# Two more products by Strassen's seven multiplications, and late roots by Heron's rule, in a two-layer graph network with an eigen-solver

## The chip, the cores and the metric

The kernel runs on one core of a Trainium2 chip. Its time is the device time of one execution in microseconds (us), and smaller is better. PE is the matrix engine (TensorE), DVE is VectorE, ACT is ScalarE, POOL is GpSimd, SP is the engine that issues most of the DMAs.

## The reference

Everything is float32. `x` holds 64 graphs of 256 nodes with 256 features, and all share one 256x256 matrix `adj`. Two blocks follow each other, each with a layer norm and a relu in front and a residual sum behind.

```python
# layer 0
G = adj * adj
h = relu(layernorm(x))
h = relu(G @ (h @ W1))        # W1 256x512
h = relu(G @ (h @ W2))        # W2 512x1024
x = x + G @ (h @ W3)          # W3 1024x256
# layer 1
h = relu(layernorm(x))
A  = adj;  deg = A.sum(0) + A.sum(1) - diag(A);  dinv = deg ** -0.5
_, U = eigh(dinv[:, None] * (diag(deg) - A) * dinv[None, :])
h = relu((U.T @ h) @ V1 + b1)  # V1 256x128
x = x + U @ (h @ V2 + b2)      # V2 128x256
```

The second block needs all eigenvectors U of one symmetric 256x256 matrix, which depends on `adj` alone.

## The kernel before

**Layer 0** goes over 32 pairs of graphs. For a pair q the class `Layers` issues, on PE: `first` (G^T h), `widened` (W1), `spread_by_seven` (G), `third_by_seven` (W2, as a 2x2 block product with Strassen's seven products in place of eight), `fourth` (W3: 32 matmuls of 128x128 by 128x256 into two held PSUM banks, over the eight 128-row blocks of `s2`), `last` (G on the result `p3`), then, after the residual sum and the second layer norm, `turn_rows` (eight transposes) and `for_layer1` (h V1, called hw). The residual row and hw of each pair are spilled to DRAM. ACT copies the products out of PSUM and does the relus (`rectify` does those on `s2`), POOL issues DMAs that add in flight and computes the norms' inverse roots with its power operation. `products` writes the order of a pair's work down; parts of neighbouring pairs are interleaved in it.

**The eigen-solver** (`Eigen`) runs beside layer 0 as one long dependent chain, mostly on DVE, with help of ACT, POOL and PE: a Householder reduction to tridiagonal form until about 1300 us, leaves of 16 by QL steps until about 1660, and then four levels of divide and conquer (32, 64, 128, 256) until about 2137. In each level `rational_steps` finds the new eigenvalues, as many in parallel as there are columns: a starting value, then `ROOT_STEPS` = 5 rational steps, each with a quadratic formula whose square root `power(dq, dq, 0.5)` is computed on POOL (`rdq` in the profile), six per level and 24 in all:

```python
            self.ts(dq, dq, 1e-36, OP.max)
            self.power(dq, dq, 0.5)
            self.tt(b, b, dq, OP.add)
            self.recip(b, b)
```

**The order on the engines** is made when the program is built. Layer 0 and layer 1 are generators (`streams`), the solver calls its instructions one by one, and `Pace` holds a model of each engine's clock. When the solver has an instruction for PE or ACT, `Pace.run` first issues whatever of the streams can begin before that instruction is due. The order of PE and ACT is then fixed, and in the levels that of POOL too (`pool_too`, in `join`). A stream can yield a condition (a lambda), and it goes on only when that holds in the plan. On the chip each engine works off its list in order and waits with semaphores for data.

**Layer 1** begins when U is there. A flag from the solver is read, a branch is taken (`mend`, which would repeat the last phase of the solver), and then for each pair: hw and the row are fetched by SP, `to_vectors` computes U^T hw (four matmuls of 128x128 by 128x256 per pair), DVE adds b1, ACT applies the relu, POOL makes `xb`, the row plus U's row sums times b2; `from_vectors` multiplies with U and `finish` with V2, DVE adds `xb` and SP writes the output. `layer1_of` runs these three pairs deep.

Most lines of the profile carry L210, the line of the helper that issues all calls, so groups are told apart by tile names: `s` is `s2` (numbers are left out of names), `L_gnn_W` a weight, `forms` and `sums` belong to the W2 product.

Of the kernel before, what the change touches and what calls it, by code (L numbers as in the profile page):

```python
# [29 lines left out]
H = 2  # L30
PAIRS = 32
SEVEN_FROM = 1
FLAG_US = 3.5
LN_EPS = 1e-5
EPS = 2.0**-24
# [6 lines left out]
QL_QUICK = 32  # L42
QL_LATE = 30
ROOT_STEPS = 5
ROOT_LAST = 2.0**-8
EXP_STEPS = [64, 32, 16, 8, 4, 2, 1]
MANT_BITS = 23
# [238 lines left out]
class Eigen:  # L286
# [947 lines left out]
    def rational_steps(self, n, kd, zsum, zown, znxt, acc, s, gap, half, y, bs, rb):  # L1234
# [33 lines left out]
        for step in range(ROOT_STEPS):  # L1268
            self.tt(x, y, s, OP.mult)
            for h in range(H):  # L1270
                self.ts(bs[:, h, :], kd[:, h, :], x[:, h : h + 1], OP.subtract)
            self.recip(rb, bs)
            if wide:
                for i in range(3):
                    for h in range(H):
                        a = rb if i == 0 else t
                        c = zsum if i == 0 else rb
                        self.stt(
                            t[:, h, 0:n], a[:, h, :] if i == 0 else a[:, h, 0:n], 1.0, c[:, h, :],
                            OP.mult, OP.mult, accum=sums[:, i, h : h + 1],  # L1280
                        )
            else:
                tv = t.rearrange("p h n -> p (h n)")[:, 0 : 3 * H * n].rearrange("p (i h n) -> p i h n", i=3, h=H)
                self.tt(tv[:, 0], rb, zsum, OP.mult)
                self.tt(tv[:, 1], tv[:, 0], rb, OP.mult)
                self.tt(tv[:, 2], tv[:, 1], rb, OP.mult)
                nc.vector.tensor_reduce(
                    sums.rearrange("p i h -> p (i h)"), tv.rearrange("p i h n -> p (i h) n"), AX.X, OP.add
                )
            self.tt(w, gap, y, OP.subtract)  # L1290
            self.tt(dd, w, y, OP.subtract)
            self.tt(m, y, w, OP.mult)
            self.tt(ms, m, s, OP.mult)
            self.ts(low, y, 2.0**-5, OP.mult)

            fv, g, b, c, c1, c2, dq = (f(k) for k in ("rf", "rg", "rb1", "rc", "rc1", "rc2", "rdq"))
            self.stt(fv, sums[:, 0], 1.0, s, OP.add, OP.mult)
            self.tt(g, fv, m, OP.mult)
            self.tt(c, fv, dd, OP.mult)
            self.tt(c1, dd, sums[:, 1], OP.mult)  # L1300
            self.tt(b, m, sums[:, 1], OP.mult)
            self.tt(c1, fv, c1, OP.subtract)
            self.tt(c2, ms, sums[:, 2], OP.mult)
            self.tt(b, b, c, OP.add)
            self.tt(c1, c1, c2, OP.subtract)
            self.tt(c2, b, b, OP.mult)
            self.tt(c1, c1, g, OP.mult)
            self.stt(dq, c1, 4.0, c2, OP.mult, OP.add)
            self.ts(dq, dq, 1e-36, OP.max)
            self.power(dq, dq, 0.5)  # L1310
            self.tt(b, b, dq, OP.add)
            self.recip(b, b)
            self.tt(g, g, b, OP.mult)
            if step == ROOT_STEPS - 1:
                size, near = f("rsz"), f("rnear")
                self.ts(size, g, -1.0, OP.mult)
                self.tt(size, size, g, OP.max)
                self.ts(near, y, ROOT_LAST / 2, OP.mult)
                self.tt(near, size, near, OP.is_le)
            self.stt(y, g, -2.0, y, OP.mult, OP.add)  # L1320
            self.tt(y, y, low, OP.max)
            self.tt(y, y, half, OP.min)
# [456 lines left out]
class Layers:  # L1779


    def __init__(self, tc, ctx, ap, gt2, u, ut):
# [17 lines left out]
        self.parts = [self.s1.rearrange("p m b f -> p (m b) f")[:, 1:4], forms[:, 0:3]]  # L1800
        self.y2 = self.forms.rearrange("p a c n -> p (a c n)")[:, 0:2048].rearrange("p (c n) -> p c n", c=4)
        self.sums = pool.tile([P, 3, 2, 512], F32, name="sums")
        self.s2 = pool.tile([P, 2, 4, 2, N], F32, name="s2")
        self.p3 = pool.tile([P, H, 2 * N], F32, name="p3")
        self.x1 = pool.tile([P, H, 2, N], F32, name="x1")
# [35 lines left out]

    def open1(self, ctx):

        self.io1 = ctx.enter_context(self.tc.tile_pool(name="l1_io", bufs=5))
        self.op = ctx.enter_context(self.tc.tile_pool(name="l1_out", bufs=3))
        self.wp1 = ctx.enter_context(self.tc.tile_pool(name="l1_work", bufs=4))
        self.ps1 = ctx.enter_context(self.tc.tile_pool(name="l1_psum", bufs=4, space=PSUM))
# [61 lines left out]
        return self.wp.tile([P, H, 2, N], F32, tag=tag, name=tag)  # L1909

    def streams(self):
        return Stream(self.products()), Stream(self.rows())

    def products(self):

# [2 lines left out]
        for q in range(PAIRS):  # L1918
# [1 line left out]
            if q == SEVEN_FROM:  # L1920
                yield from self.fold_weights()
            last = self.last(q - 1) if q > 0 else iter(())
            for part in self.third_by_seven() if seven else self.third():
                if part is None:
                    yield from next(last, ())
                else:
                    yield part
            if more:
                yield from self.first(q + 1)
                yield from self.widened(0)  # L1930
                yield from self.widened(1)
            forms = iter(())
            if more:
                forms = self.spread_by_seven() if q + 1 >= SEVEN_FROM else self.spread_in_turn()
            turned = iter(())
            if q > 0:
                yield lambda: q - 1 in self.h1
                turned = self.turn_rows()
                for _ in range(8):
                    yield next(turned)  # L1940
            step = next(forms, iter(()))
            if seven:
                yield from self.rectify(0)
            for _ in range(4 if more else 0):
                yield next(step)
            yield from turned
            yield from step
            products = self.fourth()
            yield from next(products)
            if seven:  # L1950
# [138 lines left out]
    def fold_weights(self):  # L2089
# [14 lines left out]
        self.lhs = {1: a[0, 0], 2: a[0, 1], 3: f3, 4: a[1, 1], 5: f5, 6: f6, 7: a[1, 0]}  # L2104
        self.rhs = {1: 0, 5: 1, 4: 2, 7: 3, 3: 4, 2: 5, 6: 6}

    def seventh(self, ps, k, jj, start=False):
        for i in range(2):
            at = (2 * jj + i) * P
# [7 lines left out]
                    skip_group_check=not start,  # L2117
                )

    def third_by_seven(self):  # L2120


        act = self.nc.scalar.activation
# [15 lines left out]
        for k, to in ((1, 1), (6, 2), (5, 0)):  # L2139
            for jj in range(2):  # L2140
                yield from product("u", jj, k, s2[:, jj, to])
            if k != 5:
                yield None
        yield from part("z", 0, 7, 0)
        yield from part("y", 0, 2, 1)
# [19 lines left out]
    def fourth(self):  # L2165
# [26 lines left out]
        for m in range(H):  # L2192
            yield second_half(m)

    def last(self, q):

        nc, x1 = self.nc, self.x1
        def rows(m):
            ps = self.bank()
            yield from self.products_of(  # L2200
                ps, [(self.gt2[:, h, m * P : (m + 1) * P], self.p3[:, h, :]) for h in range(H)]
# [47 lines left out]
    def turn(self):  # L2249

        nc = self.now
        nc.vector.tensor_reduce(self.u1, self.u, AX.X, OP.add)
        for h in range(H):
            nc.vector.tensor_scalar(self.ub2[:, h, :], self.b2, self.u1[:, h : h + 1], None, OP.mult)

    def fetch(self, q):
        hw = self.io1.tile([P, H, 2, P], F32, tag="hw", name="hw1")
        x1 = self.io1.tile([P, H, 2, N], F32, tag="x", name="x1")
        yield self.nc.sync.dma_start(out=hw.rearrange("p h b k -> p (h b k)"), in_=self.spilled_hw[q])
        yield self.nc.sync.dma_start(out=x1.rearrange("p h b f -> p (h b f)"), in_=self.spilled[q])  # L2260
        self.fetched[q] = x1, hw

    def to_vectors(self, q):

        nc = self.nc
        x1, hw = self.fetched.pop(q)
        z = self.wp1.tile([P, H, 2, P], F32, tag="z", name="z")
        ps = self.bank1()
        for m in range(H):
            yield from self.products_of(  # L2270
                ps[:, m * N : (m + 1) * N],
                [
                    (self.u[:, h, m * P : (m + 1) * P], hw[:, h].rearrange("p b k -> p (b k)"))
                    for h in range(H)
                ],
            )
        yield nc.vector.tensor_tensor(
            z.rearrange("p h b k -> p (h b) k"),
            ps.rearrange("p (g k) -> p g k", k=P),
            self.b1.unsqueeze(1).to_broadcast([P, H * 2, P]),  # L2280
            OP.add,
        )
        s = self.wp1.tile([P, H, 2, P], F32, tag="s", name="s")
        yield nc.scalar.activation(s, z, AF.Relu)
        xb = self.wp1.tile([P, H, 2, N], F32, tag="xb", name="xb")
        for b in range(2):
            yield nc.gpsimd.tensor_tensor(xb[:, :, b, :], x1[:, :, b, :], self.ub2, OP.add)
        self.mid[q] = s, xb

    def from_vectors(self, q):  # L2290

        s, xb = self.mid.pop(q)
        g = self.wp1.tile([P, 2 * N], F32, tag="g", name="g")
        ps = self.bank1()
        for b in range(2):
# [1 line left out]
                ps[:, b * N : (b + 1) * N], [(s[:, m, b, :], self.ut[:, m, :]) for m in range(H)]  # L2297
            )
        yield self.nc.scalar.copy(g, ps)
        self.end[q] = g, xb  # L2300

    def finish(self, q):
        nc = self.nc
        g, xb = self.end.pop(q)
        out = self.op.tile([P, H, 2, N], F32, tag="out", name="out")
        for m in range(H):
            ps = self.bank1()
# [5 lines left out]
            yield nc.vector.tensor_tensor(flat(out)[:, m, :], flat(xb)[:, m, :], ps, OP.add)  # L2313
            yield nc.sync.dma_start(out=self.view(self.ap["out"], q)[:, m], in_=out[:, m])

    def layer1_of(self, ahead=3):

        ready = lambda q: lambda: q in self.through
        for i in range(PAIRS + 2 + ahead):
            if i < PAIRS:  # L2320
                yield ready(i)
                yield from self.fetch(i)
            if 0 <= i - ahead < PAIRS:
                yield from self.to_vectors(i - ahead)
            if 0 <= i - ahead - 1 < PAIRS:
                yield from self.from_vectors(i - ahead - 1)
            if 0 <= i - ahead - 2:
                yield from self.finish(i - ahead - 2)

    def layer1(self, pace):  # L2330


        with self.tc.manual_schedule():
            self.turn()
            self.due = True
            self.fetched, self.mid, self.end = {}, {}, {}
            pace.streams = *pace.streams, Stream(self.layer1_of())
            pace.finish()


# [66 lines left out]
```

## Time and profile before

| | us |
|---|---|
| median of 3 runs (lowest, highest) | 2330.01 (2328.76, 2330.02) |
| the profiled execution | 2329.52 |
| its span, from the first to the last instruction | 2327.7 |
| PE busy in the span | 2276.4 |
| DVE busy | 1972.7 |
| ACT busy | 1224.3 |
| POOL busy | 720.1 |

The granted clock of TensorE is 0.999 of full speed over the span. A PE share is the time in which matmuls run; the weight load (PEld) overlaps them. Each float32 matmul leaves two records, so a count of x16 in a row of matmuls is eight matmuls. A releaser (`<-`) is what an engine waited for last.

### The profile page before, as it was taken

To read this page: it belongs to the slowest core of one execution; us is meant where nothing else is said; L and a number is where in the kernel's file an instruction comes from. 1 tells how busy PE (TensorE), PEld (TensorE's weight loads), DVE (VectorE), ACT (ScalarE), POOL (GpSimd) and SP (SyncE) were. 2 spreads that over 40 slices of the span, in tenths; PEclk is the share of its full clock that TensorE was granted. 3 is DMA by queue.
4 is the path that set the end of the run, shared out by engine and by line. 5 is a ranking of instruction groups with operands and counts; after the bars stand their busy time and mean duration, and the time that the engine had idled before them with its cause. 6 is when DMAs were issued, how large, how long until landed. Compare 5 with 4: busy or idle time off the path is not lost. (4 is left out here: it accounts for less than half of the span.)

```text
span 2327.7 us, 40756 instructions
## 1 busy us (share of the span) xinstructions
PE 2276.4 (98%) x10686; PEld 1850.2 (79%) x10686; DVE 1972.7 (85%) x12008; ACT 1224.3 (53%) x3015; POOL 720.1 (31%) x1978
## 2 busy tenths in 40 slices
PE   7999999999999999999999899999999999999999
PEld 4688888788778878888888778778888888787888
DVE  7989999999998999999999999999887787873343
ACT  4355655455554555556655356555555555544322
POOL 3445544455554223222222011111111111111543
PEclk9999999999999999999999999999999999999999
DMA  3123232223223222323323123333332222224776
GB/s 127 23 60 73 64 69 60 55 60 69 65 60 70 60 63 56 72 65 69 73 60 73 37 64 73 73 68 65 73 73 64 66 65 58 63 55 114 235 254 202
DMA packets 70622, 183.25 MB, mean 79 GB/s; under 512 B 7920, under 2 KB 29040, under 8 KB 70384
## 3 DMA queue, kind: packets, MB, share of 16 engines
q0 software_dynamic: 18000, 89.92, 20.3%
q1 hardware_dynamic: 52384, 90.67, 11.3%
q8 instruction: 86, 1.41, 0.2%
q14 instruction: 152, 1.25, 0.2%
HBM read 65.48 MB, written 41.94 MB: 46 GB/s over the span
## 5 line engine op out<-in xcount | busy, mean ns | idle before, releaser
L210 PE MATMUL bank<-forms,L_gnn_W 128*128 128x256 f32 (+2 forms) x2104 | 489.1, 381 | 0.0
L210 PE MATMUL bank<-L_gnn_W,s 128*128 128x256 f32 (+1 forms) x2096 | 472.4, 375 | 4.1 <-ACT s L210 3.1
L210 PEld LDWEIGHTS bank<-forms,L_gnn_W 128*128 128x128 f32 x2104 | 391.2, 191 | 60.6 <-issue 11.7
L210 PEld LDWEIGHTS bank<-L_gnn_W,s 128*128 128x128 f32 x2096 | 389.4, 190 | 56.9 <-ACT s L210 6.1
L210 ACT ACTIVATE s<-bank 128x512 f32<-128x512 f32 (+1 forms) x485 | 281.2, 582 | 218.0 <-PE bank L210 214.7
L210 PE MATMUL bank<-forms,sums 128*128 128x256 f32 (+1 forms) x1524 | 348.3, 374 | 0.0
L210 PEld LDWEIGHTS bank<-forms,sums 128*128 128x128 f32 x1524 | 283.4, 190 | 58.2 <-issue 23.7
L210 PE MATMUL bank<-gt,s 128*128 128x256 f32 (+1 forms) x1062 | 247.2, 372 | 1.1 <-ACT s L210 0.7
L210 PE MATMUL bank<-L_gnn_W,y 128*128 128x512 f32 (+1 forms) x530 | 231.0, 579 | 2.9 <-ACT y L210 2.9
L210 PEld LDWEIGHTS bank<-gt,s 128*128 128x128 f32 x1062 | 191.9, 190 | 24.7 <-ACT s L210 2.6
L210 ACT ACTIVATE forms<-bank 128x512 f32<-128x512 f32 x217 | 127.8, 590 | 118.3 <-PE bank L210 117.6
L210 POOL COPY m<-xr 128x1 f32<-128x1 f32 x254 | 58.6, 231 | 390.3 <-DVE xr L210 390.1
L210 PEld LDWEIGHTS bank<-L_gnn_W,y 128*128 128x128 f32 x530 | 97.6, 190 | 99.8 <-issue 87.3
L210 DVE SCALAR_TENSOR_TENSOR A<-xr,wc,A 128x255 f32<-128x255 f32 (+63 forms) x381 | 140.5, 369 | 0.0
L210 DVE SCALAR_TENSOR_TENSOR A<-wr,q,A 128x255 f32<-128x255 f32 (+63 forms) x381 | 139.2, 366 | 0.0
L210 ACT ACTIVATE junk<-xr 128x254 f32<-128x254 f32 (+63 forms) x127 | 45.9, 362 | 171.5 <-DVE xr L210 169.2
L210 ACT ACTIVATE junk<-x,nm 128x256 f32<-128x256 f32 x256 | 128.6, 502 | 3.8
L210 PE MATMUL bank<-p,gt 128*128 128x512 f32 (+3 forms) x266 | 122.8, 576 | 0.0
L210 PE MATMUL bank<-gt,h 128*128 128x256 f32 (+1 forms) x518 | 119.9, 381 | 0.1
L210 ACT ACTIVATE junk<-x 128x256 f32<-128x256 f32 x256 | 105.8, 413 | 25.6 <-DMA x<-in_x_dram 21.9
L210 DVE SCALAR_TENSOR_TENSOR r<-A,xr 128x255 f32<-128x255 f32 (+63 forms) x381 | 117.9, 310 | 0.1
L210 PEld LDWEIGHTS bank<-gt,h 128*128 128x128 f32 x518 | 97.8, 192 | 14.0 <-ACT h L210 0.8
(614 smaller groups left out, 4643.9 us busy)
## 6 DMA issues: line engine op xcount, KB each, us to landing
x<-x SPq DMA_DIRECT2D x64, 512.0 KB, 3.6
forms<-forms POOLq DMA_DIRECT2D x31, 768.0 KB, 6.0
s<-s POOLq DMA_DIRECT2D x31, 768.0 KB, 5.8
s<-forms POOLq DMA_DIRECT2D x31, 768.0 KB, 6.0
x<-in_x_dram SPq DMA_DIRECT2D x64, 256.0 KB, 3.0
x<-in_x_dram POOLq DMA_DIRECT2D x32, 512.0 KB, 5.4
hw<-hw SPq DMA_DIRECT2D x64, 256.0 KB, 2.8
out_dram<-out SPq DMA_DIRECT2D x64, 256.0 KB, 2.2
```

The costliest lines, as they stand in the source:

```text
L210: return op.call(*op.args, **op.kwargs)
```

## The change

There are three parts.

1. **W3 by seven, pairs 25 to 29** (`W3_SEVEN = range(24, 29)`, counted from 0). The product of `s2` (1024 deep) with W3 is taken as 2x2 blocks. `fold_last` forms four combinations of W3's blocks on GpSimd, three of them into tiles that are free until U exists (`u`, `ut`) and into the new tile `rest`, the fourth in place of a block of W3; `unfold_last` loads that block again for the 30th pair. `fourth_by_seven` issues seven products of eight 128-column matmuls each. The combinations of `s2` are made by `sides` on GpSimd, eight sums of 128x512 per pair, and three sums of 128x256 assemble `p3`. `sides` is a third stream for the planner, tied to the PE stream by conditions. `third_by_seven` gets one reordering, and `rectify` moves within the pair.
2. **U^T hw by seven.** `turn` forms combinations of U's blocks on DVE once; `differ` forms, for two pairs at a time, four differences of hw of 128x256 on GpSimd; `to_vectors` issues seven matmuls where eight were, and DVE reads each of the seven results with its sum. The fetches of hw and of rows are separated, and the `xb` sums and the differences are a stream of their own (`sides1`).
3. **Heron's rule.** In the last three of the five rational steps of each level, the square root is replaced by one step of Heron's rule from |b|, on DVE: (dq/|b| + |b|)/2.

The diff, cut to its core:

```diff
+W3_SEVEN = range(24, 29)
+NEAR_STEPS = 2
...
-            self.power(dq, dq, 0.5)
-            self.tt(b, b, dq, OP.add)
+            if step < NEAR_STEPS:
+                self.power(dq, dq, 0.5)
+                self.tt(b, b, dq, OP.add)
+            else:
+
+                self.stt(c, b, -1.0, b, OP.mult, OP.max)
+                self.ts(c, c, 1e-18, OP.max)
+                self.recip(c2, c)
+                self.tt(dq, dq, c2, OP.mult)
+                self.tt(dq, dq, c, OP.add)
+                self.stt(b, dq, 0.5, b, OP.mult, OP.add)
             self.recip(b, b)
...
     def streams(self):
-        return Stream(self.products()), Stream(self.rows())
+        return Stream(self.products()), Stream(self.rows()), Stream(self.sides())
...
+            if q in W3_SEVEN:
+                one, two, seven_, six, five, four, three = self.fourth_by_seven(q)
+                for _ in range(4):
+                    yield next(one)
+                yield from self.for_layer1(q - 1)
+                yield from next(forms)
+                for _ in range(4):
+                    yield next(two)
+                yield from self.rectify(1)
+                self.said.add((q, "relu1"))
+                for part in (next(forms), one, two, seven_, six, next(forms), five, four, three):
+                    yield from part
+                continue
...
+    def fold_last(self):
...
+        for out, x, y in (
+            (t1, b[0, 1], b[0, 0]),
+            (t2, b[1, 1], t1),
+            (t3, b[1, 1], b[0, 1]),
+            (t4, b[1, 0], t2),
+        ):
+            yield tt(out, x, y, OP.subtract)
...
+    def fourth_by_seven(self, q):
...
+        yield product(1, one, 0, p3[:, 0])
+        yield product(2, two, 0, parts[:, 0])
+        yield product(7, two, N, parts[:, 2], "s3")
+        yield product(6, one, 0, p3[:, 2], "s2")
+        yield product(5, one, 0, p3[:, 3])
+        yield product(4, two, N, parts[:, 1])
+        yield product(3, one, 0, p3[:, 1], "s4")
+
+    def sides(self):
+
+        tt = self.nc.gpsimd.tensor_tensor
...
+        yield from self.fold_last()
+        for q in W3_SEVEN:
+            for out, x, y, op, jj, need, mark in (
+                (s1, a21, a22, OP.add, 0, "relu0", None),
+                (a21, a11, a21, OP.subtract, 0, None, None),
+                (s1, a21, a22, OP.add, 1, "relu1", None),
+                (a21, a11, a21, OP.subtract, 1, None, "s3"),
+                (a11, s1, a11, OP.subtract, 0, 1, None),
+                (a11, s1, a11, OP.subtract, 1, None, "s2"),
+                (a12, a12, a11, OP.subtract, 0, 2, None),
+                (a12, a12, a11, OP.subtract, 1, None, "s4"),
+            ):
...
+                yield tt(out[:, jj], x[:, jj], y[:, jj], op)
...
+            yield lambda: (q, 2, "out") in self.said
+            yield tt(p3[:, 0], p3[:, 0], parts[:, 0], OP.add)
+            yield lambda: (q, 4, "out") in self.said
+            for a in (2, 3):
+                yield tt(p3[:, a], p3[:, a], parts[:, a - 1], OP.add)
...
+    def differ(self, q):
+        b = self.corner(q)
+        t = self.of[q] = self.wp1.tile([P, 4, N], F32, tag="t", name="t", bufs=2)
+        for out, x, y in ((0, b[1], b[0]), (2, b[3], b[1]), (1, b[3], t[:, 0]), (3, b[2], t[:, 1])):
+            yield self.nc.gpsimd.tensor_tensor(t[:, out], x, y, OP.subtract)
...
+        def first():
+            yield from take(1, one, 0, z[:, 0, 0])
+            yield from take(2, two, 0, z[:, 0, 0], z[:, 0, 0])
+
+        def second():
+            yield from take(6, one, 0, z[:, 0, 1])
+            yield from product(7, two, N)
+
+        def third():
+            yield from take(5, one, 0, z[:, 1, 1])
+            yield tt(z[:, 1, 1], row(two[:, N:512]), z[:, 1, 1], OP.add)
+
+        def fourth():
+            yield from take(4, two, N, z[:, 0, 1], z[:, 0, 1])
+            yield from relu(0)
+            yield from take(3, one, 0, z[:, 1, 0])
+            yield from relu(1)
```

The tiles that hold fetched rows go from five buffers to four, those for hw from five to six.

## The prediction

> **What bounds the kernel now.** I read the page's busy shares first, then the busy table by stage, then the waits, then single rows of the timeline.
>
> ```profile
> PE 2276.4 (98%) x10686; PEld 1850.2 (79%) x10686; DVE 1972.7 (85%) x12008; ACT 1224.3 (53%) x3015; POOL 720.1 (31%) x1978
> ```
>
> TensorE (PE) is idle for 51 of 2327.7 us, so only less PE work, or less waiting of PE, shortens the run. By stage (columns: window, its length, then busy us of PE, weight load, DVE, ACT, POOL, clock, DMA share, GB/s):
>
> ```profile
> 0.00:1300.00 1300.00, 1271.53 (x6096) 1023.65 (x6097) 1203.41 (x7580) 722.22 (x1848) 524.84 (x1721) 1.00 0.28 66
> ...
> 1660.00:2142.00 482.00, 477.56 (x2199) 390.38 (x2197) 365.97 (x1671) 262.65 (x604) 71.42 (x104) 1.00 0.29 66
> 2142.00:2327.70 185.70, 178.12 (x824) 154.18 (x824) 67.27 (x99) 49.07 (x91) 81.89 (x68) 1.00 0.71 234
> ```
>
> The third window is that of the levels of the eigen-solver, where the new W3 products lie: PE idles 4.4 us of 482 and POOL is free for 411. The last window is layer 1: PE is busy for 178 of 186. In the levels the waits are, on PE and on DVE (us in total, times, longest):
>
> ```profile
> PE psB L210 <- DVE m L210: 1.2, 1, 1.2
> ...
> DVE rb L210 <- POOL rdq L210: 45.4, 24, 7.7
> DVE A L210 <- POOL rn L210: 16.5, 4, 4.7
> ```
>
> So the eigen chain waits long for GpSimd powers (`rdq`), while PE hardly ever waits for that chain: PE has other work in front of it. What the chain gains is worth nothing by itself; what it loses beyond its small lead, PE pays in full.
>
> **W3 by seven, PE's part.** The length of a matmul is read from starts (a matmul leaves two records):
>
> ```profile
> 2073.86 3.62 PE L210 MATMUL bank<-L_gnn_W,s 128*128 128x256 f32 x16
> 2077.32 1.95 PE L210 MATMUL bank<-L_gnn_W,x 128*128 128x128 f32 x16
> 2079.10 1.89 PE L210 MATMUL bank<-gt,s 128*128 128x256 f32 x8
> ```
>
> Eight matmuls of 256 columns take 2077.32 - 2073.86 = 3.46 us, 0.4325 each; eight of 128 columns 1.78 us, 0.2225 each. Half as wide costs 51%, not 50%, so little of the eighth is lost. A pair has 32 x 0.4325 = 13.84 us before and 7 products x 8 x 0.2225 = 12.46 after: -1.38, and -6.9 for five pairs.
>
> **U^T hw by seven, PE's part.** Two pairs have 8 matmuls of 256 columns before and 7 after: -0.4325 for each of 16 couples, -6.9. Together -13.8: 2329.5 (the profiled run; the median of three is 2330.0) becomes 2315.7 if every wait stays. The changed PE order, summed with such rows, gives -13.6 in all.
>
> **U^T hw, the other engines.** A couple takes PE 23 x 0.4325 = 9.9 us. GpSimd has 4 `xb` sums of 1.30 and 4 new ones of half the size, about 0.65: 7.8. DVE has 7 reads of 256 columns at about 0.42 and 4 output adds of 0.69: 5.7. PE stays the bound. The DMA moves the same 2.5 MB per couple, in 9.9 instead of 10.4 us: the window's 234 GB/s become 245, and single slices of the page already show 254. Products that share a bank stand 1.7 to 2.2 us apart in the PE order, against 0.42 for DVE's read. I take these at nothing; if the cover fails, 0.5 us per couple, 8 in all. At the start PE waits 1.73 us for hw now; with two pairs fetched earlier I take 1.1: -0.6.
>
> **The sums on GpSimd.** A pair gets 8 sums of 128x512 and 3 of 128x256. The nearest row is the same operation on the same size:
>
> ```profile
> L210 POOL TENSOR_TENSOR xb<-x,ub 128x512 f32<-128x512 f32 x64 | 80.0, 1297 | 71.6 <-issue 67.3 <-DVE out L210 4.3
> ```
>
> At 1.30 and about 0.65 that is 8 x 1.30 + 3 x 0.65 = 12.4 us of POOL per pair. Not all of it is hidden. Summing the changed PE order, PE comes to product 7 of the 25th pair at 1697.3. Its left side needs the second rectify (ACT, 1.05 + 0.62 us; from the ACT rows free from 1693.6, so done at 1695.3) and then two sums, 2.6 us, with hand-offs 1698.1: a wait of 0.8. Product 6 needs two more sums, 2.6, against the 1.78 of product 7: again about 0.7. Products 5, 4 and 3 come later than their sums. So 1.5 us per pair, 7.5 for five: as much as the eighth saved there. If the sums are stretched, `scale` on POOL shows by how much: 1.00 us beside small DVE work, 1.39 at 1799.6 beside wide DVE operations. At 1.8 us per sum both waits grow by about 1.0: 3.6 per pair, 18 in all.
>
> **The folds of W3.** Three sums of 128x512 stand in the POOL order before the copy `m` of the second Householder step:
>
> ```profile
> 26.88 0.18 POOL L210 COPY m<-xr 128x1 f32<-128x1 f32 x1 [2.27 <-DVE xr L210]
> ```
>
> POOL was idle for 2.27 us there; 3 x 1.30 = 3.9 make the copy 1.6 us late, and up to 3.1 with the stretch. PE's order is tied to this chain up to some 800 us (PE idles about 11 us per 100 there), so that is paid: +1.6. The fourth fold, at about 1655, is once 1.3 us beside a long QL chain: nothing, at most 1.3.
>
> **Heron's rule.** Twelve of 24 powers go. A kept one costs the chain a wait of 0.81 and an add of 0.2; the replacement is three dependent small DVE operations at 0.2 and up to 0.25 of side work: 0.2 to 0.4 saved each, 2.4 to 5 us. On top go the stalls of these powers behind other POOL work: the twelve waits sum to 16.8, of which 12 x 0.81 is the power itself, so 7.1. The chain gains 9.5 at least. Of this PE sees only its one wait of 1.2 (`psB`). In the changed PE order the solver's products stand 0.3 (first level) to 4.1 us (flag) earlier, counted in PE work, so 4 us of Heron's gain is spoken for; the rest is lead. The kept powers now queue behind sums, 1.3 each for some ten: 13 at most, most of which lead and gain cover. I take 0.
>
> **Sum.** 2329.5 - 13.8 + 7.5 + 1.6 - 1.2 - 0.6 = 2323.0.
>
> **What speaks against it.** DVE and POOL do hold each other up in this trace. POOL's one-element `q` here takes 0.69 us and ends only after the DVE addition with two inputs in SBUF is over; elsewhere the same form runs in 0.24:
>
> ```profile
> 18.92 0.69 DVE L210 TENSOR_TENSOR sums<-L_gnn_W 128x512 f32<-128x512 f32 x1
> ...
> 19.02 0.69 POOL L210 TENSOR_SCALAR q<-xr 128x1 f32<-128x1 f32 x1
> ```
>
> In the other direction the one long POOL operation beside dependent DVE work does not hold it:
>
> ```profile
> 1734.95 1.00 POOL L210 TENSOR_TENSOR scale<-v,rsqrt 128x4 f32<-128x4 f32 x1
> 1735.01 0.16 DVE L210 TENSOR_TENSOR rg<-rg,rb 128x2 f32<-128x2 f32 x1
> 1735.21 0.16 DVE L210 SCALAR_TENSOR_TENSOR cur<-rg,cur 128x2 f32<-128x2 f32 x1
> ```
>
> DVE steps on every 0.2 us within that power. But a power of four columns mostly computes, and a sum of 512 columns streams; the `xb` sums ran only beside DVE work that reads PSUM. So the trace leaves it open. The Trainium skill (SBUF — State Buffer, section "SBUF: two separate sides") states that the port pair which GpSimd shares with VectorE is an exclusive lock for a whole instruction, against a VectorE operation with two SBUF inputs, whoever starts first. The row of `q` agrees and the row of `scale` does not; by that rule the estimate would be that of the third case below, without it 2323.
>
> **Cases.**
> 1. As summed: 2323, from 2317 (GpSimd's sums come a little earlier than worked out) to 2327 (kept powers or layer 1 cost some). Chance 0.45, most of it faster. For it: the rows of `xb` and `scale`.
> 2. The sums stretch beside DVE's wide work, DVE keeps its pace: 2315.7 + 18 + 3.1 - 1.8 = 2335, and anything from 2327 up. Chance 0.2. For it: `scale` at 1.39; against: that was one of many at 1.0 to 1.2.
> 3. Slower: each sum holds DVE's two-input operations, and the eigen chain, not PE, sets the pace of the levels. Sorting the DVE rows of the five stretches by operands, 46 to 66% of the time is in such operations, say 55%: 5 x 12.4 x 0.55 = 34 us. Heron's 9.5 and PE's own 7.5 of waiting (in which the chain catches up) go off: +17, 2340 (at 46% 2334, at 66% 2347). It decides from some 29 us held, that is 46% of the 62 us of sums. Chance 0.27.
> 4. The sums never make PE wait: 2315.7 - 1.8 + 1.6 = 2315.5. Chance 0.08. Against: product 7's own sums, for which PE has only 3.5 us of work behind the rectify.
>
> That the change does not do what it says can be left out for PE: the instruction lists show the seven products.
>
> **How the numbers follow.** A measurement of this kernel can tell about 0.2%, 4.7 us, from no change: faster is below 2325.3, slower above 2334.7. Faster: 0.38 of case 1 and all of case 4, 0.46. Same: 0.07 of case 1, 0.09 of case 2, 0.03 of case 3, 0.19. Slower: 0.11 of case 2 and 0.24 of case 3, 0.35. The time is that of case 1; the range runs from 2316 to case 3's middle, 2341. Case 1's own range is 2317 to 2327.
>
> **What would show it.** In the changed profile: PE busy about 2262 to 2263 us (2276 before); waits of PE for POOL's `s` of 0.8 and 0.7 us in each of five pairs; POOL sums of `s` at a mean of 1.3 (case 2: 1.8); twelve `rdq` left, and their DVE waits nearer to 25 us than 45; DVE's 128x256 additions in the levels still at 0.42 (case 3: PE waits for DVE's `m` and `zc`, or DVE gaps as long as POOL's sums); layer 1 some 7 us shorter than 185.7. I am wrong if PE's work does not fall by 13 to 14 us, if PE waits for the solver in the levels for over 5 us, or if layer 1 does not shorten.

## The result: slower by 1%, and what the profile after shows

The changed kernel takes 2351.04 us (median of six runs, 2349.08 to 2351.79) beside 2327.86 us of the kernel before (six runs): ratio 1.0096, 95% interval 1.0086 to 1.0107. The forecast was 2323, the range 2316 to 2341.

The span grew by 21.0 us, from 2327.7 to 2348.7. The page's first row of the changed kernel, then the stages from the levels on (window, its length, busy us of PE, weight load, DVE, ACT, POOL, clock, DMA share, GB/s):

```profile
PE 2271.4 (97%) x10912; PEld 1850.4 (79%) x10912; DVE 2044.3 (87%) x12152; ACT 1229.2 (52%) x3040; POOL 826.8 (35%) x2089
```

```profile
1660.00:2160.00 500.00, 481.17 (x2466) 399.30 (x2465) 412.20 (x1734) 269.71 (x630) 127.50 (x147) 0.99 0.28 64
2160.00:2348.70 188.70, 171.38 (x782) 146.53 (x781) 90.15 (x183) 46.91 (x91) 126.04 (x132) 0.97 0.69 230
```

PE's idle time in the levels went from 4.4 to 18.8 us, DVE's busy time there from 366 to 412, and the clock is below 1.00 in both stages. The solver's flag shows how the 21 us divide. Its matmul, before and then in the changed kernel:

```profile
2136.93 0.28 PE L210 MATMUL psC<-bad,ones 128*128 128x1 f32 x2
```

```profile
2155.70 0.28 PE L212 MATMUL psC<-bad,ones 128*128 128x1 f32 x2
```

It started 18.8 us later, and from there to the end it is 193.0 us where it was 190.8. So the levels lost 18.8 us, and layer 1, which should have become 6.9 us shorter, became 2.2 longer.

What PE waits for in the levels now (us in total, times, longest):

```profile
PE bank L212 <- ACT rest L212: 5.8, 5, 1.6
PE psA L212 <- DVE m L212: 5.4, 3, 2.6
PE psB L212 <- DVE m L212: 3.6, 2, 2.0
PE bank L212 <- ACT s L212: 1.9, 2, 1.1
...
PE bank L212 <- POOL s L212: 0.6, 1, 0.6
```

`psA` and `psB` are the solver's products: PE now waits for the eigen chain, 9.0 us against 1.2. It hardly waits for GpSimd's sums. The sums of 512 columns themselves took the time that was forecast, 1.31 us in two of three groups and 1.44 in the third (`y<-s`); those of 256 columns took 0.88 and not 0.65 (columns: count, then busy us, mean ns, idle before):

```profile
L212 POOL TENSOR_TENSOR s<-s 128x512 f32<-128x512 f32 x20 | 26.1, 1313 | 0.8
L212 POOL TENSOR_TENSOR y<-s 128x512 f32<-128x512 f32 x10 | 14.4, 1438 | 48.8 <-ACT s L212 48.8
L212 POOL TENSOR_TENSOR s<-y,s 128x512 f32<-128x512 f32 x10 | 13.0, 1313 | 0.7 <-PE bank L212 0.7
L212 POOL TENSOR_TENSOR p<-p,rest 128x256 f32<-128x256 f32 x15 | 13.0, 878 | 9.1 <-ACT rest L212 9.1
```

The reason stands in the timeline rows of the first pair with sums. First DVE's rows of the kernel before, at the first level's additions:

```profile
1696.74 0.42 DVE L210 TENSOR_TENSOR dn<-dn,f 128x256 f32<-128x256 f32 x1
1697.08 0.42 DVE L210 TENSOR_TENSOR al<-zn,rtn 128x256 f32<-128x256 f32 x1
1697.41 0.42 DVE L210 TENSOR_TENSOR be<-tau,rtn 128x256 f32<-128x256 f32 x1
```

and the same instructions in the changed kernel, with POOL's rows of that time (a row marked x2 is two sums):

```profile
1698.98 2.72 POOL L212 TENSOR_TENSOR s<-y,s 128x512 f32<-128x512 f32 x2
...
1700.50 1.49 DVE L212 TENSOR_TENSOR dn<-dn,f 128x256 f32<-128x256 f32 x1
...
1701.67 2.85 POOL L212 TENSOR_TENSOR s<-s 128x512 f32<-128x512 f32 x2
1701.91 1.48 DVE L212 TENSOR_TENSOR al<-zn,rtn 128x256 f32<-128x256 f32 x1
...
1703.32 1.48 DVE L212 TENSOR_TENSOR be<-tau,rtn 128x256 f32<-128x256 f32 x1
```

An addition of 0.42 us, one every 0.34, has become one every 1.41: DVE and POOL go in turns, one DVE addition per POOL sum. Each sum takes some 1.07 us from the chain while the chain has such work. POOL pays as well where it comes second, as this sum beside back-to-back DVE additions does (1.27 is the rule):

```profile
1695.06 2.62 POOL L212 TENSOR_TENSOR y<-s 128x512 f32<-128x512 f32 x1 [4.62 <-ACT s L212]
```

In layer 1 one wait holds the loss. POOL's row and PE's row of it:

```profile
2176.49 0.88 POOL L212 DMA_DIRECT2D x<-in_x_dram  x1
...
2191.48 3.43 PE L212 MATMUL bank<-ut,s 128*128 128x256 f32 x8 [9.55 <-ACT s L212]
```

The DMA that adds the last pair's residual row is queued on POOL behind four `xb` sums, though its row was ready at 2169.8. It landed 9.2 us after its issue (5.6 before); the norm's first ACT operations stand in ACT's order ahead of the relu that PE needs, so PE stood for 9.55 us. The four matmuls after it then took 3.3 us where 1.73 is the rule, because the clock was low (one us each, the clock in the third column from the right):

```profile
2191.00:2192.00 1.00, 0.52 (x1) 0.50 (x2) 0.02 (x1) 0.95 (x2) 1.00 (x2) 0.50 0.94 344
2192.00:2193.00 1.00, 1.00 (x4) 0.74 (x3) 0.83 (x2) 0.00 (x0) 1.00 (x2) 0.50 0.60 246
```

### The profile page after: what moved, and what is told of

Its sections match the earlier page's. It is cut to its first block, busy times and chain, and to the rows that moved or that the text cites. A ratio compares the mean times of both kernels' runs of the same rounds, so it can differ in the third digit from the quotient of the medians.

```text
span 2348.7 us, 41525 instructions
## 1 busy us (share of the span) xinstructions
PE 2271.4 (97%) x10912; PEld 1850.4 (79%) x10912; DVE 2044.3 (87%) x12152; ACT 1229.2 (52%) x3040; POOL 826.8 (35%) x2089
## 3 DMA queue, kind: packets, MB, share of 16 engines
q8 instruction: 88, 1.44, 0.3%
## 5 line engine op out<-in xcount | busy, mean ns | idle before, releaser
L212 PE MATMUL bank<-L_gnn_W,s 128*128 128x256 f32 (+1 forms) x2100 | 440.3, 359 | 8.8 <-ACT rest L212 5.8
L212 PEld LDWEIGHTS bank<-L_gnn_W,s 128*128 128x128 f32 x2100 | 368.3, 190 | 54.8 <-ACT s L212 4.8
```

The source lines that it names most:

```text
L212: return op.call(*op.args, **op.kwargs)
```

## The experiments

Each run below states what it leaves of the change. Ratios are to runs of the kernel before on the same chip (2328.1 to 2328.8 there); a difference from the changed kernel itself (2351.0) compares two chips.

For all of them I compare when DVE reaches the same instruction of the solver, in us against the profiled run of the kernel before. The first row also shows the spread between executions: runs in which nothing is changed up to that point lie between -3.4 and 0.

| DVE's landmark (time before) | changed | no W3 by seven | Heron only | sums beside | fills beside | no Heron |
|---|---|---|---|---|---|---|
| level 32 begins (1667.2) | -0.4 | -3.1 | -2.4 | -0.7 | -2.1 | +2.4 |
| level 32, roots begin (1712.0) | +8.2 | -3.1 | -2.4 | +7.9 | -1.3 | +10.9 |
| level 64 begins (1770.7) | +9.7 | -5.7 | -5.1 | +16.9 | +3.3 | +11.7 |
| level 128 begins (1878.4) | +12.2 | -6.7 | -6.1 | +21.1 | +6.2 | +17.5 |
| level 256 begins (1990.6) | +20.0 | -7.6 | -6.9 | +31.7 | +8.3 | +31.0 |
| level 256, roots done (2109.6) | +15.5 | -10.6 | -9.9 | +31.7 | +7.2 | +30.3 |
| flag read (2137.2) | +18.8 | -9.3 | -8.5 | +31.7 | +6.7 | +29.4 |

### Sums that nobody reads

```diff
+        pool = self.nc.gpsimd
+        for q in range(24, 29):
+            for i in range(8):
+                yield lambda: (q, "relu0" if i < 2 else "mid") in self.said
+                yield pool.tensor_tensor(self.rest[:, 512:1024], self.rest[:, 0:512], self.rest[:, 512:1024], OP.add)
+            for i in range(3):
+                yield pool.tensor_tensor(self.rest[:, 512:768], self.rest[:, 0:256], self.rest[:, 512:768], OP.add)
```

> The kernel before, with GpSimd sums added that nobody reads: 8 of 128x512 and 3 of 128x256 on a tile of zeros, in each of the 25th to 29th pair, at about the places of the change's sums; W3 by eight, no Heron. Theory A (hold): DVE's two-input operations come one per sum, the chain is 25 to 35 us late at the flag, 2350 to 2362. Theory C (only PE's waiting for the sums costs): nobody waits, 2328 to 2332. Theory D (GpSimd is occupied, so its powers come late): at most about 13 us, 2330 to 2343, with DVE's additions at their 0.42 us.

Measured: 2363.11 us (2362.57 to 2364.02), ratio 1.0147 (1.0130 to 1.0164). The chain is 31.7 us late at the flag, and no result of these sums is waited for. So the sums alone, on a tile of their own, cost more than the whole change lost, and the theory of PE's waiting (C) falls. The theory of late powers (D) falls too: DVE waits less for them than before, 36.7 us where it was 45.4.

```profile
DVE rb L210 <- POOL rdq L210: 36.7, 24, 7.7
```

What grew is the time inside DVE's instructions. From 1660 to the flag DVE is busy for 407.5 us where it was 365.5, with the same instructions. DVE's smallest operations are held too; these are additions of one or two columns, 0.16 us long otherwise:

```profile
1764.96 1.23 DVE L210 TENSOR_TENSOR rnear<-rsz,rnear 128x2 f32<-128x2 f32 x1
1766.11 0.15 DVE L210 TENSOR_TENSOR cur<-cur,half 128x2 f32<-128x2 f32 x1
1766.22 0.16 DVE L210 SCALAR_TENSOR_TENSOR rnear<-rnear,sv 128x2 f32<-128x2 f32 x1
1766.30 1.23 DVE L210 TENSOR_TENSOR cur<-cur,half 128x2 f32<-128x2 f32 x1
```

The long ones begin 1.34 us apart, which is the mean length of these sums (1.345). An operation of two columns moves hardly any data, so this is no shared bandwidth: it waits for a whole sum to end.

### Fills instead of sums

```diff
-                yield pool.tensor_tensor(self.rest[:, 512:1024], self.rest[:, 0:512], self.rest[:, 512:1024], OP.add)
+                yield pool.memset(self.rest[:, 0:1280], 0.0)
...
-                yield pool.tensor_tensor(self.rest[:, 512:768], self.rest[:, 0:256], self.rest[:, 512:768], OP.add)
+                yield pool.memset(self.rest[:, 0:640], 0.0)
```

> As the run with sums that nobody reads, but each sum is a fill (8 of 128x1280 and 3 of 128x640 per pair), which writes SBUF and reads nothing. Theory A in the form that only a GpSimd operation that reads SBUF holds DVE: 2328 to 2333. If any long GpSimd operation holds DVE, or if GpSimd being occupied is what costs (D): as the sums, in proportion to the length of a fill.

Measured: 2337.44 us (2336.22 to 2340.32), ratio 1.0039 (1.0025 to 1.0054). The fills occupy POOL for 59.3 us, the sums did for 65.1; the chain is 6.7 us late at the flag against 31.7. Neither form of the expectation fits exactly: most of the price goes with what the sums read, a fifth stays. The rows show both. In the middle of six fills of 1.2 us each, DVE's additions with two inputs run at their usual 0.41 every 0.33 us:

```profile
1687.83 6.27 POOL L210 MEMSET rest<- 128x1280 f32 x6
...
1689.73 0.41 DVE L210 TENSOR_TENSOR num<-num,tol 128x256 f32<-128x256 f32 x1
1690.07 0.41 DVE L210 TENSOR_TENSOR sq<-sq,fp 128x256 f32<-128x256 f32 x1
```

and a DVE operation with one input and two columns (0.16 to 0.17 otherwise) ends with a fill:

```profile
1705.30 1.08 DVE L210 TENSOR_SCALAR sv<-kcol 128x2 f32<-128x2 f32 x1
...
1705.41 0.94 POOL L210 MEMSET rest<- 128x640 f32 x1
```

The Trainium skill (SBUF — State Buffer, section "SBUF: two separate sides") states both halves: the port pair is held for whole instructions, two-input VectorE work is blocked only by GpSimd operations that read SBUF, and VectorE work in a 2-port mode by any. The sums agree with it, and so do the fills, if that TENSOR_SCALAR ran in such a mode, which the trace does not tell. The row of `scale` in the prediction does not: that power reads SBUF, and DVE's two-input operations ran inside it at 0.16 us.

### The change without W3 by seven

The diff of the change without `W3_SEVEN`, `fold_last`, `fourth_by_seven`, `sides` and their places in `products`.

> Parts 2 and 3 of the change (U^T hw by seven, Heron's rule) without part 1: W3 stays at eight products for all pairs, and nothing is summed on GpSimd in the levels. Theory A (a GpSimd sum holds DVE's operations, so the eigen chain is late): the chain is not late any more, the flag comes at 2135 to 2138 instead of 2155.7 (before: 2136.9), and layer 1 keeps its own loss from the start (9.6 us of PE waiting behind the last pair's norm): 2330 to 2334. Theory B (layer 1's loss comes only from the later flag): layer 1 shows its 7 us, 2322 to 2324. Theory C (PE's waits for the sums are what costs): as A, since they go too; this run doesn't tell A from C.

Measured: 2318.29 us (2317.96 to 2319.44), ratio 0.9957 (0.9940 to 0.9974). It was run again beside other kernels:

> Parts 2 and 3 once more, on this chip and beside the run with the earlier DMA: 2316 to 2320, ratio 0.994 to 0.997.

Measured: 2319.69 us (2318.87 to 2320.33), ratio 0.9968 (0.9956 to 0.9980). In both runs this version is faster than the kernel before, by 0.3 to 0.4%, and so than the changed one. Its levels and its layer 1, with the border at the flag's branch:

```profile
1660.00:2132.00 472.00, 469.94 (x2171) 385.20 (x2169) 370.15 (x1726) 262.15 (x602) 62.94 (x92) 1.00 0.29 66
2132.00:2316.20 184.20, 176.16 (x812) 151.97 (x812) 90.17 (x183) 47.33 (x91) 126.01 (x132) 1.00 0.71 237
```

The flag comes 9.3 us earlier than before instead of 18.8 later, PE idles 2.1 us in the levels, the clock is 1.00, and the 9.55 us wait of layer 1 is gone. From 1660 to the flag DVE is busy for 369.8 us here and for 411.9 in the changed kernel, so W3 by seven lengthens DVE's own time by 42 us and puts the flag back by 28. Theory A as I had written it, with layer 1's loss left in place, is wrong on that; theory B was right that the 9.55 us follow from the late flag. With the flag early, PE still has 22 matmuls of W3 to do behind the branch, 9.5 us (12 in the kernel before, 6 in the changed one). POOL makes its eight differences and four `xb` sums meanwhile, and the residual's DMA leaves at 2147.8, 0.5 us after its row is ready.

### Heron's rule alone, and the change without it

> Part 3 alone: Heron's rule in the last three steps of each level. The chain of the levels gets 6 to 10 us shorter in itself, but before it PE hardly waits for the chain, and PE's work is not changed: 2327 to 2330 for all theories (the plan is made anew, so the flag may come earlier with more of layer 0 left behind it). If the chain set the end of layer 0 by itself, 2320 to 2323.

Measured: 2324.36 us (2322.70 to 2331.63), ratio 0.9986 (0.9976 to 0.9996). Better than expected of a chain that PE doesn't wait for: 6.1 us of the 8.5 at the flag were won inside the levels. PE's work is the same; what went is idle time, 8.0 us from 1660 to the end beside 12.0. PE's waits for hw (1.7) and for the branch (0.7) at the start of layer 1 are gone. Some of the difference between the two profiles is chance: the kernel before ran 3.4 us at half clock at 1318, ahead of the levels, and this one none.

> Parts 1 and 2 without Heron's rule (all 24 powers stay on GpSimd). With the chain late at the flag, the chain sets the end of layer 0, and what Heron gives it counts in full: 2357 to 2361 (6 to 10 us more than the changed kernel). If Heron's gain is hidden behind PE as the prediction held, 2350 to 2352.

Measured: 2358.38 us (2356.86 to 2360.56), ratio 1.0127 (1.0110 to 1.0144). With the chain late, Heron's gain counts in full: 7.3 us between 2358.4 and 2351.0, 10.6 us at the flag (2.8 of them stand there already when level 32 begins, before any root is computed).

### U^T hw by seven alone

> Part 2 alone, U^T hw by seven: PE's work falls by 6.9 us, and nothing before the flag is touched: 2321 to 2323 (before: 2328.8 on that chip). If GpSimd's differences of hw hold DVE or come late for PE, or if the DMA can't follow: 2324 to 2330.

Measured: 2327.77 us (2325.42 to 2331.18), ratio 1.0001 (0.9992 to 1.0011). The whole 6.9 us are gone. In its trace PE waits 2.6 us for the relu behind the last pair's norm, 2.1 for hw and 2.1 for DVE's `z`, and the matmuls after the first of these take twice their time (four in 3.7 us). Beside Heron's rule the same part is worth 6.1 us (2324.4 to 2318.3).

### The order on GpSimd at the start of layer 1

In three kernels the first `xb` sums were made to wait, in the plan, for the issue of the last pair's residual DMA:

```diff
             yield self.nc.gpsimd.dma_start(out=self.x1, in_=self.ap["x"][q], accum_op=OP.add)
+            self.said.add((q, "residual"))
...
-            yield lambda: q in self.x_of and (q < 5 or q - 5 in self.gone)
+            yield lambda: q in self.x_of and (q < 5 or q - 5 in self.gone) and (PAIRS - 1, "residual") in self.said
```

> The changed kernel, with one move in GpSimd's order: the DMA that adds the last pair's residual row stands ahead of the first four sums of layer 1 (xb), not behind them. If that queueing is what makes PE wait 9.6 us for ACT at 2181 to 2191 in the changed kernel (the DMA could start at 2169.8, it started at 2176.5, and PE's clock halves after the pause): 8 to 11 us less than the changed kernel, 2340 to 2343. If the DMA is late because the fetches of layer 1 crowd it (9.2 us to landing instead of 5.6): 3 us less or nothing, 2348 to 2351.

Measured: 2345.67 us (2344.48 to 2348.59), ratio 1.0077 (1.0061 to 1.0094): 5.4 less than the changed kernel, between the two expectations.

> Parts 2 and 3, and the last pair's residual DMA ahead of the first xb sums. With Heron the flag leaves enough of layer 0 behind it, the DMA went out at 2147.8, 0.5 us after its row was ready, and PE waits 0.4 us for ACT there: 2316 to 2319, no more than 1 us apart from the run without this move.

Measured: 2325.18 us (2322.28 to 2325.67), ratio 0.9988 (0.9979 to 0.9997): 5.5 us more than the same kernel without the move on that chip, where at most 1 was expected.

> Part 2 alone, with the residual DMA ahead of the first xb sums. In part 2 alone (2327.8) PE waits 4.5 us for ACT's relu behind the last pair's norm and 2.1 for hw, and runs at half clock after that. If the DMA's place is the cause, 3 to 5 us less: 2323 to 2325. If the DMA's landing (crowded by fetches) is, 2327 to 2328.

Measured: 2330.60 us (2328.46 to 2333.16), ratio 1.0011 (1.0002 to 1.0020): 2.8 more instead of 3 to 5 less. (The 4.5 us of the expectation are three waits; the one behind the norm is 2.6.) Both misses have one cause, which the trace of the second kernel shows. The DMA does not leave earlier there: its row is ready at 2149.2, POOL stands idle for 4.93 us until then, and the four `xb` sums that used to fill that time now come behind the DMA. With them everything moves back, and the next four stand before the norm's own small operations of the last pair:

```profile
2149.46 0.90 POOL L211 DMA_DIRECT2D x<-in_x_dram  x1 [4.93 <-ACT x L211]
...
2158.12 4.95 POOL L211 TENSOR_TENSOR xb<-x,ub 128x512 f32<-128x512 f32 x4
...
2163.16 0.19 POOL L211 TENSOR_SCALAR v<-v 128x4 f32<-128x4 f32 x1
...
2166.70 0.33 PE L211 MATMUL bank<-eye,x 128*128 128x128 f32 x1 [4.02 <-ACT x L211]
```

The row's squares were summed by 2159.6, `v` waited until 2163.2, and PE 4.0 us for the normed row. Without the move the DMA left at 2148.6 and `v` ran at 2158.9. In the third kernel it is the same: the DMA at 2153.4 (2153.6 without the move), `v` at 2167.2 (2164.8), and PE waits 3.9 us for the normed row. Only the changed kernel, where the row had been ready for 6.7 us, sent its DMA earlier (2171.5 instead of 2176.5).

### One pair instead of five

```diff
-W3_SEVEN = range(24, 29)
+W3_SEVEN = range(24, 25)
```

> The changed kernel with W3 by seven for the 25th pair alone (folds as in the changed kernel, one pair of sums instead of five). Runs so far: sums that nobody reads put the chain back by 31.7 us for five pairs, 6.3 per pair; parts 2 and 3 alone run in 2318.3. One pair: chain 6 to 8 us later at the flag than there (folds 1.7, sums 6.3), PE's work 1.4 less, and less cover behind the flag: 2323 to 2330. If the price grows with all five only (a threshold), 2317 to 2319.

Measured: 2328.57 us (2327.44 to 2331.87), ratio 1.0006 (0.9996 to 1.0015): 8.9 us more than without W3 by seven (2319.7 on that chip), for 1.38 us of PE work saved. So the price begins with the first pair, and from one pair to five it grows by 22.5 us more, 5.6 a pair; by these two points no number of pairs pays, though two to four were not run. In its trace the chain stands 10.3 us later at the flag than in the run without W3 by seven. Of these 3.5 stand already before the levels, where only the folds of W3 differ, but runs with nothing changed up to there lie as far apart (3.4).

### The sums on DVE

```diff
-        tt = self.nc.gpsimd.tensor_tensor
+        tt = self.nc.vector.tensor_tensor
```

in `sides`. The folds of W3, which the expectation counts in, stay on GpSimd: `fold_last` has a `tt` of its own, and the trace shows them on POOL.

> The changed kernel with the sums of W3's products (and the folds of W3) on DVE in place of GpSimd. DVE needs 0.69 us for a sum of 128x512 and 0.42 for one of 128x256, 8 x 0.69 + 3 x 0.42 = 6.8 us per pair, and it works on the chain itself. If a GpSimd sum holds DVE for nearly its whole 1.31 us while DVE has two-input work (1.07 us measured between DVE's additions beyond their own 0.34), the price was 6 to 8 us per pair too, and moving the sums onto the chain's own engine changes little: 2343 to 2354. If holding is not the price of the sums, 5 x 6.8 = 34 us more than the changed kernel: 2375 to 2390.

Measured: 2351.20 us (2349.51 to 2353.66), ratio 1.0101 (1.0084 to 1.0118), the time of the changed kernel. All that GpSimd beside DVE spared the chain is 5.4 us at the flag: with 33.3 us of sums on DVE the flag stands 24.2 us later than before, with 66.9 us of them on GpSimd 18.8. That the totals agree to 0.2 us is chance, since the time from the flag to the end is 186.9 us here and 193.0 in the changed kernel.

## Why the prediction was wrong

**The step that failed** is the choice in the part "What speaks against it", and with it the order of the cases. Two rows spoke of the two engines together. The row of `q` (0.69 us, ending with DVE's addition) said that they exclude each other, the row of `scale` (1.00 us, with DVE running inside it) said that they don't, and I took `scale`. So the sum put at nothing what GpSimd's sums take from DVE, and let the chain keep its lead. The runs showed that DVE's two-input additions come one per sum, every 1.41 us instead of 0.34, and that sums which nobody reads put the flag back by 31.7 us. `scale` was the wrong neighbour: a power of four columns reads eight numbers per row in its 1.00 us, a sum of 512 columns reads 1024 in its 1.30. Why the power holds nothing, no run shows. The `q` row and the rule that the prediction cites from the Trainium skill agreed; the run with sums that nobody reads settles it.

**The size of the third case**, 34 us held, lies near the 31.7 at the flag without Heron, in part by luck: DVE's instructions got 42 us longer, and 10 of these came out of DVE's waits, which the case did not count. **Its sum was off**: it put 17 us on top of 2323, a figure from which the 6.9 us of W3 and the 6.9 of layer 1 were already taken off. A chain that is late sets the flag by itself, and PE's saved work before the flag then only becomes idle time. Such a case has to be summed from the flag. With the measured parts that is 2329.5 + 18.8 at the flag + 2.2 in layer 1 = 2350.5, the profiled run (2350.45); this divides up what was measured and forecasts nothing.

**PE's part of W3**: right in the rate. Sixteen records of 128 columns still start 1.78 to 1.79 us after each other. The page's PE busy fell by 5.0 and not by 13.8. Matmuls ran at half clock for 9.7 us (3.4 before), which makes them some 3 us longer. The seven products of the five pairs add up to 65.3 us of busy time and not 62.3: short waits inside a product count as busy. The rest, about 3 us, is open.

**PE's waits for the sums**: 7.5 us were forecast, 6.4 measured as idle time, so the size came out by luck: they are not the ones I named. 5.8 of them are for ACT's copy of product 2, which shares a PSUM bank with product 7 (1.04 us in four pairs, 1.62 in one), and 0.6 for POOL.

**The folds**: 1.6 us forecast. The copy `m` began 1.6 us later, as forecast (28.49 instead of 26.88). What reaches the chain had no run of its own: in the five runs with the folds level 32 begins at -0.7 to +2.4, in the eight without them at -3.4 to -0.7 and in the kernel before at 0, some 2.5 us apart on average; single runs of a group lie up to 3.4 apart, so the size is rough. The reason given, that PE idles about 11 us per 100 up to 800 us, was misread: PE is idle for 27.8 us of these 800, and 16.5 of them lie in the first 100.

**Heron's rule**: the chain's gain was put at 9.5 us, 6.1 were measured inside the levels alone and, beside the sums, 7.8 of the 10.6 at the flag. That PE sees only 1.2 of it was wrong: Heron's rule alone took 4.5 us off the median (the interval of the ratio allows 1 to 5.6). A flag that comes earlier leaves more of layer 0 for PE to do during the first fetches of layer 1. The waits that are gone there account for 2.4 us; that the whole gain comes this way is not shown.

**U^T hw, taken at nothing beyond PE's 6.9 us**, with 8 us if the cover fails. The cover that I checked was the steady state, and there it held: windows of 20 us show PE busy for all 20. At the start it failed, in the changed kernel (9.55 us) and in the run of this part alone (2.6 us). The work that hides the start is what is left of layer 0 behind the flag, which I had not counted. POOL is also fuller than worked out: a difference of 128x256 takes 0.74 us, not 0.65.

## What to carry to other kernels

Before work is given to an engine that looks idle, look for rows in which it runs beside the engine that carries the chain, and take those with the most similar access, not the most similar length; here an idle GpSimd could not add two SBUF tiles without holding up VectorE's own additions. Where a dependent chain and a full engine end nearly together, first settle which of the two is late after the change: the other's saving is then worth nothing. And a stage whose steady state is covered has still to be checked at its start, where the cover is what the stage before left over.

## What the runs showed of the hardware

A GpSimd sum that reads SBUF and a DVE operation with two SBUF inputs exclude each other for whole instructions: even two columns on DVE wait out the sum (1.23 us instead of 0.16). The GpSimd power of 128x4 is an exception: beside it DVE keeps its 0.16 us. A reciprocal of 128x256 beside the sum `y` took its usual 1.75 us, and DVE's additions of a PSUM tile in layer 1 (`z<-bank,b`) their 0.42 beside the `xb` sums. DVE's two-input additions keep their 0.41 beside a GpSimd fill, while a one-input TENSOR_SCALAR waited for the fill (1.08 instead of 0.17).

TensorE's granted clock fell to 0.50 after quite short pauses: after 2.56 us without a matmul (from 1710.7; half clock from 1713.2 to 1716.6) and after 1.96 us (from 1994.2; half clock from 1996.5 to 1999.9), but not after 2.37 us (from 1772.6). The first of these pauses, in PE's row:

```profile
1713.22 1.22 PE L212 MATMUL psA<-q,m 128*128 128x128 f32 x4 [2.56 <-DVE m L212]
```

Half clock for 3.4 us takes 1.7 from PE, so such a pause can cost nearly twice what it lasts. What decides between a pause that lowers the clock and one that does not, these traces do not settle.
